# The first attention unit of an AdaLN block: another load order, maxima between projections and values, scores beside maxima

## The chip, the cores and the metric

The kernel runs on one core of a Trainium2 chip. The core has a matrix engine (TensorE, PE in the profile; its weight loads are listed apart as PEld), a vector engine (VectorE, DVE), a scalar engine (ScalarE, ACT), a general engine (GpSimd, POOL) and a queue engine that issues transfers (SyncE, SP). Each works through its own list of instructions in order and waits on semaphores of the others. The metric is device time in microseconds (us) of one execution; lower is better.

## What is computed

The reference is one transformer block with adaptive layer norm, on x of 4 batches, 1024 tokens, width 256, in float32. Cut to what matters:

```python
mod = (silu(c) @ wmod).reshape(4, 6, 1, 256)          # sa, ca, ga, sb, cb, gb
h = layernorm(x) * (1 + ca) + sa
Q, K, V = split(h @ W_qkv.T + b_qkv)                  # 16 heads of 16
attn = softmax(Q @ K.T / 4 + causal)                  # 1024 x 1024 for each head
x = x + ga * (merge(attn @ V) @ W_o.T + b_o)
h = layernorm(x) * (1 + cb) + sb
x = x + gb * moe(h)                                   # 8 experts, top 2, silu
```

The gates ga and gb are pushed away from zero to at least 0.25 in magnitude. The change lies wholly in the beginning of the attention of the first batch.

## The kernel before

**Units and steps.** The attention runs in 16 units, four per batch, each of four heads. A head has 16 channels, padded to 32 rows, so four heads fill the 128 rows of `qT` and `kT`, and four matmuls on 32 rows each can run side by side in the array. Row 16 of each group of 32 in `qT` holds the row maximum of the scores, and `kT` holds -1 there, so a score matmul already subtracts the maximum. There are three pairs of `qT`, `kT`, used in turn.

For each unit the kernel first needs maxima, then scores. Maxima come in 12 steps (`m_steps`): steps 0 to 3 are the diagonal blocks of the first half of the queries, of 512, 384, 256 and 128 keys; steps 4 to 7 take the second half against the first 512 keys; steps 8 to 11 are the diagonal of the second half. Each step is four matmuls (one per head) and four reductions on DVE. Scores also come in 12 steps (`s_steps`): four matmuls, masks on the diagonal, four exponentials on ACT, and, one step later, four products with the values (`av_step`).

In the steady loop (from L1078) a score step of unit u stands beside a maxima step of unit u+1: after each score matmul comes one maximum matmul (`m_step`, L797). There, the causal mask of a maximum is added on DVE by the fused operation of L816. `m_alone` (L835) is the form for maxima with no scores beside them: four matmuls of L848, then the mask added by PE (L854, `unit` times `qmask`), then plain reductions (L856). Nothing in it prevents the list of instructions from putting each head's mask directly behind that head's matmul, and in the first step it is laid down so.

**The start.** SP issues the two halves of x of batch 0 (L132), then wq, wk, the biases, wv, and later the other batches; ACT's queue issues the condition `sc` and the first third of the modulation's weights, `wm[0]` (L608). POOL builds constants, zeroes the three `qT`, copies wq and wk out of their padded form (L653), writes ones into both value tiles (L657), and scales the query bias (L1043). ACT fills the three `kT` (L651). DVE takes layer-norm statistics (L44, L45) tile by tile; `modulate` (L670) multiplies on PE (L676), and DVE copies the result to `modT` (L680) and adds one for the scale (L681). `ln_pieces` then gives: square root on ACT (L50), a few small DVE operations (L51 to L57), normalization of half the tokens (`xna`, L67), transposes on PE (L76), and the modulated result `hT` on ACT (L77). `xna` has one buffer.

`qk_pieces` makes projections of 256 tokens (L766) and copies them with bias on ACT (L771); column half 0 serves units 0 and 1, half 1 units 2 and 3. `spread(u)` (L779) moves projected heads into `qT` and `kT` by nine transfers on SP. `modulate_rest` (L683) computes the other two thirds of the modulation on PE (L692), copied by DVE (L693) and written to DRAM. `v_pieces` makes values of 128 tokens (L741) and adds the bias on DVE (L745). `max_rows(u, half)` (L822) transposes the finished maxima, copies them on ACT (L828) and sends them into row 16 of `qT` (L829).

**The order written out by hand** (L1039 to L1076): modulation; the layer norm of batch 0; eight projection pieces; `spread(0)`; `modulate_rest`; eight more pieces; `spread(1)`; maxima steps 0 to 3 of unit 0; a value piece; `max_rows(0, 0)`; maxima steps 4 to 7 with the other value pieces; then four times a maxima step 8 to 11 followed by a score step 0 to 3 with its own four matmuls (`four_heads`); `max_rows(0, 1)`; then maxima steps 0 to 3 of unit 1, each with a layer-norm piece of batch 1 from the list `todo`. The steady loop enters unit 0 at step 4. All PSUM tiles of this part except one come from seven banks in turn.

`in_order` (L214) pins an instruction to its place in the program's order; without it the list of an engine may be laid down otherwise.

Of the kernel before, what the change touches and what calls it, by code (L numbers as in the profile page):

```python
# [18 lines left out]
P = 128  # L19
# [42 lines left out]
def normalized(nc, pool, x_b, mv, rs, half, tag):  # L62

    xn = pool.tile([P, 4, D], F32, tag=f"xn{tag}", name=f"xn{tag}")
    for i in range(4):
        t = 4 * half + i
        nc.vector.tensor_scalar(  # L67
            xn[:, i, :], x_b[:, t, :], mv[:, t, 0:1], rs[:, t : t + 1], ALU.subtract, ALU.mult
        )
    return xn  # L70
# [10 lines left out]
def adaln_block_kernel(  # L81
# [46 lines left out]
    x_view = x.rearrange("b (t p) d -> b p t d", p=P)  # L128
    out_view = out.rearrange("b (t p) d -> b p t d", p=P)
    out_rows = out.rearrange("b t d -> (b t) d")  # L130
    for h in range(2):
        nc.sync.dma_start(out=xs[0][:, 4 * h : 4 * h + 4, :], in_=x_view[0, :, 4 * h : 4 * h + 4, :])  # L132

    ident = ctile([P, P], "ident")
    make_identity(nc, ident)
# [438 lines left out]
    with ExitStack() as actx:  # L574
# [29 lines left out]
        def load_modulation(n, eng):  # L604
            for dc in range(NDC):
                eng.dma_start(out=wm[n][dc], in_=wmod[dc * P : (dc + 1) * P, 512 * n : 512 * (n + 1)])

        load_modulation(0, nc.scalar)  # L608

        padded = []  # L610
        for name, w in (("qc", wq), ("kc", wk)):
# [35 lines left out]


        for i in range(3):
            nc.gpsimd.memset(qTs[i], 0.0)  # L650
            nc.scalar.copy(kTs[i], extra.to_broadcast([P, T]))  # L651
            if i < 2:
                nc.gpsimd.tensor_copy(  # L653
                    (wq_s, wk_s)[i].rearrange("p c (h d) -> p c h d", d=DH), padded[i][:, :, :, 0:DH]
                )
        for v in vaug:
            nc.gpsimd.memset(v[:, :, :, DH:HW], 1.0)  # L657
        zrows = dnp.tile([4, T], F32, tag="zrows", name="zrows")
# [11 lines left out]
        def modulate():  # L670

            nc.scalar.activation(sc, sc, AF.Silu)
            ps = bank("ps_m")[:, 0 : 4 * B].rearrange("p (n b) -> p n b", b=B)
            for n in range(4):
                for dc in range(NDC):
                    nc.tensor.matmul(  # L676
                        ps[:, n, :], wm[0][dc][:, n * P : (n + 1) * P], sc[:, dc, :],
                        start=(dc == 0), stop=(dc == NDC - 1),
                    )
            nc.vector.tensor_copy(modT, ps)  # L680
            nc.vector.tensor_scalar(scale1[:, 0:2, :], modT[:, 2:4, :], 1.0, None, ALU.add)  # L681

        def modulate_rest():  # L683
# [30 lines left out]
        def ln_pieces(b):  # L714
            def begin():
                st["ln", b], pieces = layer_norm_pieces(nc, small, xs[b], eps, "a")
                for f in pieces:
                    f()
                st["hT", b] = htp.tile([P, NDC, T], F32, tag="hT", name="hT")

            def piece(half, dc):
                def run():
                    if dc == 0:
                        st["xn", b] = normalized(nc, xnp, xs[b], *st["ln", b], half, "a")
                    transposed(
                        nc, misc(), st["xn", b], dc, ident,
                        st["hT", b][:, dc, half * 512 : (half + 1) * 512],
                        scale1[:, dc, b : b + 1], modT[:, dc, b : b + 1],
                    )

                return run

            out = [piece(h, dc) for h in range(NH) for dc in range(NDC)]
            return [lambda f=out[0]: (begin(), f())] + out[1:]
# [100 lines left out]
        def m_alone(u, i):  # L835

            qt, kb = m_steps[i]
            half = qt // 4
            last = kb == half
            n = (qt % 4 + 1) * P if last else 512  # L840
            kind = ("mx", u, half) if last else ("mf", u)
            if kind not in st:
                st[kind] = mxp.tile([P, 4, 4], F32, tag=kind[0], name=kind[0])
            pss = []
            for j in range(4):
                pss.append(bank("ps_max"))
                r = HW * j
                nc.tensor.matmul(  # L848
                    pss[j][:, 0:n], qTs[u % 3][r : r + HW, qt * P : (qt + 1) * P],
                    kTs[u % 3][r : r + HW, kb * 512 : kb * 512 + n], start=True, stop=not last,  # L850
                )
            if last:
                for ps in pss:
                    nc.tensor.matmul(ps[:, n - P : n], unit, qmask, start=False, stop=True)  # L854
            for j, ps in enumerate(pss):
                nc.vector.tensor_reduce(st[kind][:, j, qt % 4 : qt % 4 + 1], ps[:, 0:n], AX.X, ALU.max)  # L856

# [177 lines left out]
            for k, f in enumerate(av_step(*av)):  # L1035
                soon.append((step + 3 + 2 * k, f))


        modulate()  # L1039
        ln0, keys0 = ln_pieces(0), qk_pieces(0, 0)  # L1040
        for f in ln0:
            f()
        nc.gpsimd.tensor_scalar(bq_s, bq_s, SCALE, None, ALU.mult)  # L1043
        for f in keys0 + [spread(0), modulate_rest] + qk_pieces(0, 1) + [spread(1)]:
            f()
        values = deque(v_pieces(0))
        for i in range(4):
            m_alone(0, i)
        values.popleft()()
        max_rows(0, 0)()  # L1050
        for i in range(4, 8):
            m_alone(0, i)
            while len(values) > 7 - i:
                values.popleft()()
        blank_rows()
        st["rest"] = ln_pieces(1) + qk_pieces(1, 0), v_pieces(1) + qk_pieces(1, 1)
        todo.extend(st["rest"][0][:10])
        gates.extend(gate_pieces(0)[0])

        def four_heads(u, i):  # L1060

            pts = weigh(i, [s_step(u, i, j) for j in range(4)], True)
            if pending is not None:
                finish(pending)
            return u, i, pts

        for i in range(8, 12):
            m_alone(0, i)
            pending = four_heads(0, i - 8)
        nc.vector.tensor_tensor(st["mx", 0, 1], st["mx", 0, 1], st["mf", 0], ALU.max)  # L1070
        max_rows(0, 1)()
        for i in range(4):
            m_alone(1, i)
            todo.popleft()()
        todo.appendleft(max_rows(1, 0))
        step = 4  # L1076

        for u in range(NU):  # L1078
# [22 lines left out]
            for i in range(4 if u == 0 else 0, len(s_steps)):  # L1101
# [10 lines left out]
                    sends.extend(loads)  # L1112
                if (b, qd, i) == (B - 1, 1, 4):
                    gates.extend(weights)
                pts, scores = [], []

                if u + 1 == NU:
                    pending = four_heads(u, i)
                for j in range(4 if u + 1 < NU else 0):
                    scores.append(s_step(u, i, j))  # L1120
                    m_step(u + 1, i, (j + 2) % 4)
                    if j % 2:
                        pts.extend(weigh(i, scores[j - 1 :], j == 1))

                    if j == 1 and pending is not None:
                        finish(pending)
                if u + 1 < NU:
                    pending = u, i, pts
                    if m_steps[i] == (4, 0) and u > 0:
                        todo.appendleft(max_rows(u + 1, 0))  # L1130

                if gates:
                    gates.popleft()()
# [179 lines left out]
```

## Time and profile before

| what | us |
|---|---|
| median of 3 runs (lowest, highest) | 1100.63 (1099.53, 1101.1) |
| the profiled execution, its own time | 1096.32 |
| its span, first to last instruction | 1094.4 |
| PE busy | 1047.4 (96%) |
| DVE busy | 752.1 (69%) |
| ACT busy | 530.5 (48%) |
| POOL busy | 241.3 (22%) |

The profile is of one execution. The page gives busy time by engine, 40 slices of the span (27.4 us each) with the share of busy time in tenths, the clock that was granted to PE in tenths of full speed, the transfers, and the costliest groups of instructions by line of the code. Two readings are needed here. A busy PE is not a PE at its peak: matmuls overlap, and four matmuls on 32 rows each in one microsecond count no more than one. And the slices are too coarse for a start of some 100 us, so the order of time and the table of stretches are used: each line of the first gives start, duration, engine, line of the code, operation, output and input, count, and in brackets how long the engine had stood idle and for whom.

Where the start stands in that order:

| us | event |
|---|---|
| 4.95 | first layer-norm statistics |
| 7.37 | first modulation matmul |
| 20.51 | first transposes of normalized tokens |
| 58.80 | the run of value projections begins |
| 71.95 | first score matmul |
| 83.67 | transposes of the second half's maxima |

The mean granted clock over the execution is 0.979 of full speed.

### The profile page before, as it was taken

What the parts mean: (1) busy time and instruction counts of PE and PEld (TensorE: products, weight loads), DVE (VectorE), ACT (ScalarE), POOL (GpSimd) and SP (SyncE); (2) the same over time, 40 slices, a digit from 0 to 9 for tenths busy, and PEclk for the clock granted to TensorE, in tenths of its full rate; (3) what the DMA queues carried; (4) which work ended last, traced back from release to release, by engine and by line L of the source; (5) the groups of instructions that cost most, each with busy time, mean ns of one, the idle gap of its engine ahead of it and who ended that gap; (6) DMA issues with size and microseconds to landing.
All of it is one profiled execution on the core that took longest, in us unless ns stands there. A gap on an engine that the chain in (4) does not pass through costs nothing. (4 is left out here: it accounts for less than half of the span.)

```text
span 1094.4 us, 23062 instructions
## 1 busy us (share of the span) xinstructions
PE 1047.4 (96%) x8202; PEld 589.2 (54%) x8202; DVE 752.1 (69%) x2326; ACT 530.5 (48%) x1153; POOL 241.3 (22%) x233
## 2 busy tenths in 40 slices
PE   3999999999999999999999999999799999999994
PEld 3554434444444353444445444443277888889884
DVE  5766767667777868767786778786246777666662
ACT  3224655566655455665545555444632254445540
POOL 4000010000000001330000133113213574454444
PEclk9898999999999999999999999989999999999997
DMA  8220111101102110231202113001458966443432
GB/s 274 46 55 7 31 27 37 30 17 38 30 21 75 37 40 15 74 72 40 59 15 42 45 52 100 26 22 50 142 180 265 352 154 146 78 65 64 74 63 24
DMA packets 68690, 81.61 MB, mean 75 GB/s; under 512 B 19480, under 2 KB 50072, under 8 KB 68448
## 3 DMA queue, kind: packets, MB, share of 16 engines
q1 hardware_dynamic: 54720, 62.73, 21.0%
q0 software_dynamic: 13296, 16.89, 8.7%
q8 instruction: 64, 1.05, 0.4%
q10 hardware_dynamic: 560, 0.53, 0.1%
q14 instruction: 50, 0.41, 0.1%
HBM read 45.11 MB, written 24.93 MB: 64 GB/s over the span
## 5 line engine op out<-in xcount | busy, mean ns | idle before, releaser
L888 ACT ACTIVATE pt<-ps_s 128x512 f32<-128x512 f32 (+3 forms) x768 | 334.3, 489 | 321.3 <-PE ps_s L883 206.7
L805 PE MATMUL ps_max<-kT,qT 32*128 32x512 f32 (+3 forms) x1408 | 387.9, 540 | 1.3 <-DVE mx L816 0.7
L867 PE MATMUL ps_s<-qT,kT 32*128 32x512 f32 (+3 forms) x1536 | 365.2, 539 | 2.7 <-DVE qc L535 2.1
L867 PEld LDWEIGHTS ps_s<-qT,kT 32*128 32x128 f32 x1536 | 127.9, 185 | 164.7 <-issue 70.3
L812 DVE TENSOR_REDUCE mf<-ps_max 128x1 f32<-128x512 f32 x240 | 154.2, 685 | 54.6 <-PE ps_max L805 51.2
L900 PE MATMUL av<-pt,vaug 128*32 128x512 f32 (+3 forms) x1536 | 164.6, 497 | 2.1 <-ACT ot L908 1.0
L816 DVE CUSTOM_DVE_ANT_0 unused<-ps_max,cmask,mf 128x512 f32<-128x512 f32 (+3 forms) x240 | 131.6, 548 | 46.7 <-PE ps_max L805 23.2
L932 POOL TENSOR_TENSOR oc<-oc,rec 64x512 f32<-64x512 f32 x32 | 40.8, 1274 | 540.7 <-DMA rec<-inv 423.8
L805 PEld LDWEIGHTS ps_max<-kT,qT 32*128 32x128 f32 x1408 | 142.0, 184 | 24.6 <-DVE mx L816 10.2
L816 DVE CUSTOM_DVE_ANT_0 unused<-ps_max,cmask 128x512 f32<-128x512 f32 (+3 forms) x224 | 109.9, 491 | 59.4 <-PE ps_max L805 34.0
L564 POOL DMA_INDIRECT out_dram<-y,xb x67 | 106.5, 1590 | 124.4 <-DVE gs L526 39.9
L547 PE MATMUL ps_h<-xt,wa 128*128 128x256 f32 (+1 forms) x608 | 123.6, 355 | 1.1 <-DVE xt L535 1.1
L558 PE MATMUL ps_y<-wb,hs 128*128 128x256 f32 x536 | 122.8, 379 | 1.0 <-ACT hs L551 1.0
L547 PEld LDWEIGHTS ps_h<-xt,wa 128*128 128x128 f32 x608 | 102.5, 191 | 11.6 <-DVE xt L535 1.3
L558 PEld LDWEIGHTS ps_y<-wb,hs 128*128 128x128 f32 x536 | 100.6, 190 | 14.4 <-ACT hs L551 1.4
L883 PEld LDWEIGHTS <-qmask 128*32 128x32 bf16 (+1 forms) x1352 | 30.1, 95 | 109.4 <-issue 102.0
L526 DVE SCALAR_TENSOR_TENSOR gs<-x,share,gs 128x256 f32<-128x256 f32 x201 | 85.2, 479 | 1.0
L340 POOL DMA_INDIRECT slots<-hr,sloti x64 | 64.0, 1000 | 89.5 <-ACT sloti L339 52.2
L551 ACT ACTIVATE hs<-ps_h 128x512 f32<-128x512 f32 x67 | 39.8, 597 | 87.3 <-PE ps_h L547 85.8
L563 DVE TENSOR_TENSOR y<-ps_y,gs 128x256 f32<-128x256 f32 x67 | 26.0, 420 | 73.2 <-PE ps_y L558 66.8
L883 PE MATMUL ps_s<-unit,qmask 128*32 128x128 bf16 (+1 forms) x1352 | 72.9, 226 | 0.0
L900 PEld LDWEIGHTS av<-pt,vaug 128*32 128x32 f32 x1536 | 34.1, 110 | 53.6 <-issue 39.4
(223 smaller groups left out, 988.1 us busy)
## 6 DMA issues: line engine op xcount, KB each, us to landing
w_s<-in_w_dram SPq DMA_DIRECT2D x16, 512.0 KB
xb<-slots SPq DMA_DIRECT2D x29, 259.0 KB
qT<-qc SPq DMA_DIRECT2D x64, 64.0 KB
kT<-kc SPq DMA_DIRECT2D x64, 64.0 KB
oc<-ot SPq DMA_DIRECT2D x128, 32.0 KB
rec<-inv SPq DMA_DIRECT2D x32, 128.0 KB
out_dram<-x SPq DMA_DIRECT2D x8, 512.0 KB
wa<-in_w_dram SPq DMA_DIRECT2D x8, 512.0 KB
```

The costliest lines, as they stand in the source:

```text
L340: sent = nc.gpsimd.indirect_dma_start(out=slots, out_offset=bass.IndirectOffsetOnAxis(ap=at, axis=0), in_=hr[:, t, :], in_offset=None,).ins
L526: nc.vector.scalar_tensor_tensor(gs[:, j, :], gb[:, b, :], share[:, j, b : b + 1], gs[:, j, :], ALU.mult, ALU.add)
L547: nc.tensor.matmul(ps[:, k, :], w[:, dc, fc * P : (fc + 1) * P], xt[:, dc, :], start=(dc == 0), stop=(dc == NDC - 1),)
L558: nc.tensor.matmul(ps[:, j, :], hs[:, fc, j * P : (j + 1) * P], w[:, fc, :], start=(fc == 0), stop=(fc == NFC - 1),)
L564: added = nc.gpsimd.indirect_dma_start(out=out_rows, out_offset=bass.IndirectOffsetOnAxis(ap=xb[:, j, D : D + 1].bitcast(I32), axis=0), in ...
L805: nc.tensor.matmul(ps[:, 0:n], qTs[u % 3][r : r + HW, qt * P : (qt + 1) * P], kTs[u % 3][r : r + HW, kb * 512 : kb * 512 + n], start=True, ...
L812: nc.vector.tensor_reduce(st["mf", u][:, j, qt - 4 : qt - 3], ps, AX.X, ALU.max)
L816: nc.vector.tensor_tensor_reduce(out=unused[:, 0:n], in0=ps[:, 0:n], in1=cmask[:, 512 - n : 512], scale=1.0, scalar=st["mf", u][:, j, qt - ...
L867: nc.tensor.matmul(ps[:, 0:n], kTs[u % 3][r : r + HW, kt * P : (kt + 1) * P], qTs[u % 3][r : r + HW, qb * 512 + r0 : (qb + 1) * 512], star ...
L883: nc.tensor.matmul(ps[k : k + w, 0:P], qmask[:, k : k + w], unit, start=False, stop=True)
L888: nc.scalar.activation(pt[:, 0:n], ps[:, 0:n], AF.Exp)
L900: nc.tensor.matmul(av[HW * j : HW * (j + 1), r0:512], vaug[b % 2][:, kt, 4 * qd + j, :], pts[j][:, 0 : 512 - r0], start=(kt == 0), stop=(k ...
```

## The change

Loads: x's first half goes first; `wm[0]` moves from ACT's queue to SP, between the halves of x.

Engines: the copies of wq and wk move from POOL to ACT, the first between the modulation's silu and the square root; of the `kT` fills one stays ahead of the projections' copies and two are written after twelve projection pieces; the bias scaling on POOL moves forward and is pinned behind the first zeroing of `qT`. The copy of the modulation to `modT` and its scale move behind the normalization of the first half.

Order: after eight projection pieces and `spread(0)` come four more pieces, then `modulate_rest`; the last four pieces, `spread(1)` and the eight value pieces are placed between maxima steps 0 to 7 of unit 0. In `m_alone` the first mask is pinned, so that the four matmuls stand together ahead of the masks. Maxima steps 8 to 11 of unit 0 now run beside score steps 0 to 3 by a new function `both`, the body of the steady loop; they therefore use `m_step` and DVE's mask. Layer-norm pieces of batch 1 stand there too. Of unit 1's maxima, step 0 follows `max_rows(0, 1)` and steps 1 to 3 move into steps 4 to 6 of unit 0; `max_rows(1, 0)` goes to step 7.

```diff
-    for h in range(2):
+    def load_first(h):
         nc.sync.dma_start(out=xs[0][:, 4 * h : 4 * h + 4, :], in_=x_view[0, :, 4 * h : 4 * h + 4, :])
+    load_first(0)
...
-        load_modulation(0, nc.scalar)
+        load_modulation(0, nc.sync)
+        load_first(1)
...
         for i in range(3):
-            nc.gpsimd.memset(qTs[i], 0.0)
-            nc.scalar.copy(kTs[i], extra.to_broadcast([P, T]))
-            if i < 2:
-                nc.gpsimd.tensor_copy(
-                    (wq_s, wk_s)[i].rearrange("p c (h d) -> p c h d", d=DH), padded[i][:, :, :, 0:DH]
-                )
+            in_order(nc.gpsimd.memset(qTs[i], 0.0))
+            if i == 0:
+                in_order(nc.gpsimd.tensor_scalar(bq_s, bq_s, SCALE, None, ALU.mult))
...
-            nc.vector.tensor_copy(modT, ps)
+            return ps
+        def modulated(ps):
+            in_order(nc.vector.tensor_copy(modT, ps))
             nc.vector.tensor_scalar(scale1[:, 0:2, :], modT[:, 2:4, :], 1.0, None, ALU.add)
...
                         st["xn", b] = normalized(nc, xnp, xs[b], *st["ln", b], half, "a")
+                        if b == 0 and half == 0:
+                            modulated(st.pop("ps_m"))
...
-                for ps in pss:
-                    nc.tensor.matmul(ps[:, n - P : n], unit, qmask, start=False, stop=True)
+                for k, ps in enumerate(pss):
+                    mask = nc.tensor.matmul(ps[:, n - P : n], unit, qmask, start=False, stop=True)
+                    if k == 0:
+                        in_order(mask)
...
+        def both(u, i, u_max, i_max):
+            pts, scores = [], []
+            for j in range(4):
+                scores.append(s_step(u, i, j))
+                m_step(u_max, i_max, (j + 2) % 4)
+                if j % 2:
+                    pts.extend(weigh(i, scores[j - 1 :], j == 1))
+                if j == 1 and pending is not None:
+                    finish(pending)
+            return u, i, pts
+        st["ps_m"] = modulate()
+        ln0 = ln_pieces(0)
+        ln0[0]()
+        for w, w_s in zip(padded, (wq_s, wk_s)):
+            nc.scalar.copy(w_s.rearrange("p c (h d) -> p c h d", d=DH), w[:, :, :, 0:DH])
+        nc.scalar.copy(kTs[0], extra.to_broadcast([P, T]))
+        keys1 = qk_pieces(0, 1)
+        for f in ln0[1:] + qk_pieces(0, 0) + [spread(0)] + keys1[:4]:
+            f()
+        for i in (1, 2):
+            nc.scalar.copy(kTs[i], extra.to_broadcast([P, T]))
+        modulate_rest()
+        fill = deque(keys1[4:] + [spread(1)] + v_pieces(0))
+        for i in range(8):
+            m_alone(0, i)
+            for _ in range((2, 2, 2, 1, 2, 2, 1, 1)[i]):
+                fill.popleft()()
+            if i == 3:
+                max_rows(0, 0)()
...
-        for i in range(8, 12):
-            m_alone(0, i)
-            pending = four_heads(0, i - 8)
-        nc.vector.tensor_tensor(st["mx", 0, 1], st["mx", 0, 1], st["mf", 0], ALU.max)
+        for i in range(4):
+            pending = both(0, i, 0, 8 + i)
+            todo.popleft()()
         max_rows(0, 1)()
-        for i in range(4):
-            m_alone(1, i)
-            todo.popleft()()
-        todo.appendleft(max_rows(1, 0))
+        m_alone(1, 0)
...
+                pending = both(u, i, u + 1, i) if u + 1 < NU else four_heads(u, i)
+                if u == 0 and 4 <= i < 7:
+                    m_alone(1, i - 3)
+                if u + 1 < NU and i == (4 if u > 0 else 7):
+                    todo.appendleft(max_rows(u + 1, 0))
```

As the lists are laid down, ACT's is: silu, wq copy, first `kT` fill, square root, wk copy, the other two fills, `hT`; POOL's is: zeroing of the first `qT`, ones of one value tile, bias scaling, zeroing of the other two `qT`, ones of the other value tile.

## The prediction

> **What bounds the kernel now.** I read the page first, then the first 150 us in stretches of 5 us, then the order of time for 0 to 140 us, then the waits of that stretch.
>
> The page's slices show TensorE (PE) at nine tenths nearly everywhere after the first slice:
>
> ```profile
> PE   3999999999999999999999999999799999999994
> PEclk9898999999999999999999999989999999999997
> ...
> L805 PE MATMUL ps_max<-kT,qT 32*128 32x512 f32 (+3 forms) x1408 | 387.9, 540 | 1.3 <-DVE mx L816 0.7
> L867 PE MATMUL ps_s<-qT,kT 32*128 32x512 f32 (+3 forms) x1536 | 365.2, 539 | 2.7 <-DVE qc L535 2.1
> ```
>
> The two large matmul groups wait under 3 us in all, so from the steady loop on PE's queue sets the time and whatever the first unit gains or loses should arrive at the end undiminished. In the built order of the changed kernel every engine but SP is identical to before from step 8 of unit 0 on, and SP differs only in its opening loads. So I forecast one date: when PE reaches step 8 of unit 0, **113.9 us before** (a step in the order of time that begins at 113.88 with L867 and L805).
>
> How that date comes about is in the order of time (start, duration, engine, instruction):
>
> ```profile
> 11.90 0.17 DVE L680 COPY modT<-ps_m 128x16 f32<-128x16 f32 x1 [5.80 <-PE ps_m L676]
> 12.08 3.55 POOL L657 MEMSET vaug<- 128x2048 f32 x2
> 12.15 3.50 DVE L681 TENSOR_SCALAR scale<-modT 128x8 f32<-128x8 f32 x1
> 17.27 1.28 ACT L50 ACT_TABLE_LOAD   x1 [9.56 <-DVE mva L45]
> 19.95 1.38 DVE L67 TENSOR_SCALAR xna<-x,mva,rsa 128x256 f32<-128x256 f32 x4
> 24.88 1.12 PE L766 MATMUL ps_mi<-hT,wq_s 128*128 128x256 f32 x4
> 31.97 3.60 PE L692 MATMUL ps_g<-wm,sc 128*4 128x512 f32 x8
> 35.63 0.65 DVE L693 COPY mod<-ps_g 4x512 f32<-4x512 f32 x1
> 42.60 1.12 PE L848 MATMUL ps_max<-kT,qT 32*128 32x512 f32 x2
> 46.89 0.69 DVE L856 TENSOR_REDUCE mx<-ps_max 128x1 f32<-128x512 f32 x1 [1.06 <-PE ps_max L854]
> 71.96 2.48 DVE L856 TENSOR_REDUCE mx<-ps_max 128x1 f32<-128x512 f32 x4
> 93.13 1.06 PE L867 MATMUL ps_s<-qT,kT 32*128 32x512 f32 x1
> ```
>
> DVE stands for 5.80 us in front of the modulation copy while layer-norm statistics queue behind it; its next instruction, 8 elements wide, takes 3.50 us because POOL's memsets are running. Projections start at 24.88. The first maxima (42.60) go one head at a time, and then PE runs at half clock:
>
> ```profile
> 45.00:50.00 5.00, 5.00 (x15) 1.51 (x14) 2.08 (x3) 0.00 (x0) 0.00 (x0) 0.55 0.15 26
> 50.00:55.00 5.00, 5.00 (x37) 3.14 (x30) 3.83 (x11) 0.00 (x0) 0.00 (x0) 0.50 0.00 0
> 55.00:60.00 5.00, 5.00 (x18) 2.49 (x18) 1.96 (x6) 1.54 (x2) 0.00 (x0) 0.58 0.26 99
> 95.00:100.00 5.00, 5.00 (x25) 1.91 (x24) 2.67 (x6) 3.10 (x5) 0.00 (x0) 0.50 0.00 0
> ```
>
> Columns: stretch, then busy of PE, PE loads, DVE, ACT, POOL; the granted clock stands third from the end. By single microseconds the low clock lasts from 45.3 to 59.1 and from 93.3 to 100.1.
>
> **1. Loads and first layer norm: projections start at 20.2 instead of 24.9, gain 4.7.** The ring now carries x's first half, the two wm tiles, x's second half, wq, wk, 524 kB each. The DMA view of the first 62 us (1.55 us a slice) moved 178, 687, 1288, 1872, 2472 kB by 3.1, 4.65, 6.2, 7.75, 9.3 us. Before, wq ended the first 2.1 MB, 8.35 us on this curve, and its copy began at 9.19: 0.85 from byte to use. On the same curve: first half 5.0, wm 6.4, second half 7.8, wq 9.2, wk 10.5. Moving wm from ACT's queue to SP costs two issues of 0.52 there; SP's later loads wait for bytes, not issues, so nothing more. L676's 16 matmuls (7.37 to 11.87 before) end near 10, and their copy and scale (0.17 each) now lie between the two halves of `xna`, where DVE idled 1.31 for PE: hidden. The statistics run without a break: four tiles of 0.39 after 7.8, done by 9.5. ACT is later: it now holds the wq copy (POOL's row: 0.61) and one kT fill (1.03), from 9.2 to 10.8; then table load 1.28 and square root 0.30, 12.4. The wk copy and two kT fills (0.61+2×1.03) follow to 15.1, before the first `hT` falls due near 17 (`xna` to `hT` took 2.05): hidden, up to 2.7 if the normalization came earlier. Five small DVE instructions (18.90 to 19.95 before, 1.05) make it 13.5.
>
> Here a rule is weighed. POOL now waits for bq behind wk (the DMA rate dips from 9.3 to 10.85, the small pieces; about 11), then runs three memsets, 0.95+0.95+1.81, to about 15.0. The Trainium skill, "SBUF — State Buffer", on the shared port pair, says that a two-port VectorE instruction and a GpSimd one exclude each other for the whole instruction. By that, the small tensor_scalar L56 (due 12.9) waits for the memset in progress, under 1 us. The row above says more: 3.50 us spans **both** back-to-back memsets, 1.81 each. By the row it waits to 15.0 and `xna` starts at 15.3. I take the row. From `xna` to the first projection took 24.88−19.95=4.93: **S = 20.2** (18.4 with no collision).
>
> **2. From S to the first reduction.** PE: eight projection pieces (31.83−24.88=6.95), four of the next pair (3.5), L692 (3.6): S+14.05. The q/k copies into qT, kT (SP issues 31.71 to 37.90, plus some 2 to land) come at S+15, so PE can begin maxima then. DVE cannot: after the second L693 copy it needs 8.05 (35.63 to 43.69), now less two of eight statistics, 7.3. **First reduction at S+21.3.** PE idles some 3 us there, a wait the change creates; the ACT projections behind the last square root wait as well.
>
> **3. Maxima with projections and values.** Eight maxima steps and eight values: with the masks after four concurrent matmuls, a 512 step is 1.07+0.33 instead of 6.4 (42.60 to 49.00). DVE: reductions 2.48, 1.95, 1.42, 0.88, then 4×2.48, and eight value adds of 0.41. Before, at full clock, one step and one value took 2.73 (63.78 to 66.51), DVE without a gap. Sum 19.5; PE's share (four projections 3.5, values 8.5, steps 8.4, less 3.1 done early) is 17.3, beside it. DVE ends at S+40.8=61.0; before, 71.96. From S: 40.8 against 47.1, **gain 6.3**.
>
> **4. First scores beside maxima.** Before: 71.96 to 93.13, 21.2. After: four double steps. The same steps in a later unit took 12.8 (156.2 to 169.0) at PE's limit; one value product less (−1.05), four layer-norm pieces of 0.61 more (+2.4), PE starting 1.6 ahead of DVE: 12.9, and DVE's own sum is 10.6 of custom maxima and 2.9 of `xna`, equal (the mask matmuls of the maxima go, being DVE's cmask in these steps). A **new wait** follows: `max_rows(0,1)` needs DVE's last maximum, a transpose (0.28), a copy (0.24), an 8 kB DMA (issue 0.59; a similar one, inv at 114.76, released its successor at 116.2), before step 4's scores; only one maxima step (1.4) lies between. I take 3.4. Total 16.3, **gain 4.9**.
>
> **5. Steps 4 to 7.** Before 93.13 to 113.88, 20.75, of which half clock costs 3.4. After: four steps of 4.2 (105.48 to 109.68) plus three maxima steps moved in here (1.2+0.9+0.65, with waits 3.5): 20.4, **gain 0.3**.
>
> Sum 4.7+6.3+4.9+0.3 = 16.2. The rule on idle gaps speaks against this: "TensorE: Matmul & The Clock Gate" (why this matters for your kernels) says that no gap above some 3 us may stand between bursts, else half clock. The trace's granted clock shows no drop for the 8.6 us idle before 20.5, but both drops follow thin work (single-head maxima; small maxima waiting on DVE). By the rule the waits in 2 and 4 each cost a period of 6.8 us at half clock, 3.4 each; by the rows nothing. Part 3 is DVE's, so a drop there costs 17.3+3.4−19.5=1.2. I take that one, nothing in 4: **gain 15**.
>
> Against its own time of 1096.3 (span 1094.4 and 1.9 around it) the profile would show about 1081; the median of the runs shown lies 4.3 above it: **1085.5**.
>
> **Rivals.** (a) Half the gain: both new waits cost a full low-clock period, the row DMA lands a microsecond later, DVE's custom maxima fall behind by 2: 15−3.4−1−2=8.6, **1092**. For it: the waits are real; against: the steady loop, equally built, never drops.
> (b) Slower: the low clock holds through parts 3 and 4, since interleaving leaves PE waiting on DVE all along. 17.3 and 14 us of PE work double; 17.3+17.3−19.5=15.1 plus 14 is 29 lost, **1115**. It decides once more than about 32 us beyond part 3's slack run at half clock. Against: 63 to 86 us held full clock in just such DVE-paced work.
> (c) No POOL collision, clock whole: +1.8+1.2, **1082.5**.
> (d) The start is hidden anyway: batch loads (DMA busy to 27.9) hold DVE's other statistics, so only parts 3 to 5 count: 10.3, **1090**.
>
> Chances: forecast 0.50, (a) 0.15, (b) 0.09, (c) 0.14, (d) 0.09, 0.03 for no difference. Range 1080 to 1094; outside it are (b) and little else. Under 0.2% (2.2 us) a measurement cannot tell from none: faster 0.88, same 0.03, slower 0.09.
>
> **What would show it.** Right: first L766 near 20, first L856 near 41.5 and bunched in fours, step 8 near 98.5. Wrong in 1: no DVE instruction stretched beside memsets, or one longer. Wrong in 3 or 4: granted clock 0.5 between 62 and 80, or PE waiting for rows over 3 us before the first unmasked scores. The whole is wrong if step 8's gain does not reach the end.

## The result and the profile after

The changed kernel takes 1088.42 us (median of 4 runs, 1087.28 to 1089.52) against 1100.16 in the same runs for before: ratio **0.9892**, interval 0.9875 to 0.9910. It is 11.7 us faster, where the forecast was 15 and 1085.5. The profiled execution was one of the slower ones: 1089.52 us, span 1087.8.

The lines of the page that answer to those of before (the first two are 40 slices of the span; the others give count, busy time and mean, then the idle time and its releaser):

```profile
PE   5999999999999999999999999999799999999994
PEclk9899999999999999999999999899999999999998
...
L812 PE MATMUL ps_max<-kT,qT 32*128 32x512 f32 (+3 forms) x1440 | 396.5, 537 | 1.3 <-DVE mx L823 1.1
L876 PE MATMUL ps_s<-qT,kT 32*128 32x512 f32 (+3 forms) x1536 | 364.9, 538 | 3.5 <-DVE qc L538 2.1
```

The steady loop is as before; the first slice went from 3 to 5 tenths. The start in the order of time (start, duration, engine, instruction, idle time before it), first DVE's list:

```profile
14.02 1.77 DVE L56 TENSOR_SCALAR nwa<-nwa 128x8 f32<-128x8 f32 x1
...
16.02 1.38 DVE L67 TENSOR_SCALAR xna<-x,mva,rsa 128x256 f32<-128x256 f32 x4
...
24.68 0.75 DVE L44 BATCH_NORM_STATS2 sta<-x 128x6 f32<-128x256 f32 x2 [4.59 <-DMA x<-in_x_dram]
...
30.42 0.20 DVE L51 RECIPROCAL rsa<-rsa 128x8 f32<-128x8 f32 x1 [1.70 <-ACT rsa L50]
...
43.13 2.48 DVE L865 TENSOR_REDUCE mx<-ps_max 128x1 f32<-128x512 f32 x4
46.38 1.95 DVE L865 TENSOR_REDUCE mx<-ps_max 128x1 f32<-128x384 f32 x4 [0.77 <-PE ps_max L861]
50.87 1.42 DVE L865 TENSOR_REDUCE mx<-ps_max 128x1 f32<-128x256 f32 x4 [2.54 <-PE ps_max L861]
...
66.09 0.41 DVE L752 TENSOR_TENSOR vaug<-ps_mi,bv_s 128x256 f32<-128x256 f32 x1
```

then PE's:

```profile
20.95 1.77 PE L773 MATMUL ps_mi<-hT,wq_s 128*128 128x256 f32 x4
22.55 1.03 PE L773 MATMUL ps_mi<-hT,wk_s 128*128 128x256 f32 x4
...
35.67 2.65 PE L855 MATMUL ps_max<-kT,qT 32*128 32x512 f32 x8
...
43.87 2.25 PE L855 MATMUL ps_max<-kT,qT 32*128 32x384 f32 x6 [2.60 <-DVE mx L865]
...
46.45 2.02 PE L773 MATMUL ps_mi<-hT,wq_s 128*128 128x256 f32 x4
48.26 1.76 PE L773 MATMUL ps_mi<-hT,wk_s 128*128 128x256 f32 x4
...
81.71 0.66 PE L876 MATMUL ps_s<-qT,kT 32*128 32x512 f32 x1 [0.52 <-DMA qT<-rows]
...
101.94 0.69 PE L876 MATMUL ps_s<-qT,kT 32*128 32x512 f32 x1
```

and the stretches of 5 us around the low clock (the granted clock is third from the end):

```profile
40.00:45.00 5.00, 2.40 (x9) 1.32 (x9) 4.67 (x21) 1.03 (x3) 0.00 (x0) 0.79 0.49 84
45.00:50.00 5.00, 5.00 (x21) 2.91 (x16) 2.56 (x6) 0.47 (x1) 0.00 (x0) 0.53 0.15 26
```

At the very start this column can't be used. It reads 1.00 up to 22.5 us, but the four projection matmuls at 20.95 took 0.60 us each, as long as those from 46.45 on, where the column shows half clock, and the next ones 0.38. So PE ran at half speed there although the column does not show it. "Low clock" below means what the column shows.

The dates of before in the next table that are not shown yet are these:

```profile
43.92 0.69 DVE L856 TENSOR_REDUCE mx<-ps_max 128x1 f32<-128x512 f32 x1 [0.24 <-PE ps_max L854]
...
71.63 0.41 DVE L745 TENSOR_TENSOR vaug<-ps_mi,bv_s 128x256 f32<-128x256 f32 x1
...
113.88 0.69 PE L867 MATMUL ps_s<-qT,kT 32*128 32x512 f32 x1
```

PE projects 3.93 us earlier and brings its first maximum 6.93 us earlier (42.60 to 35.67). But DVE stands from 20.1 to 24.68 for batch 1's x, and its first reduction comes only 0.79 earlier (43.92 to 43.13). PE then stands for DVE, 2.60 us. The low clock, 20.5 us long in all before 110 us in the kernel before, is 6.8 us here (43 to 50). Four stages make up the gain at step 8 of unit 0, where PE begins at 101.94 instead of 113.88:

| stage | before | after | gain |
|---|---|---|---|
| to DVE's first reduction | 43.92 | 43.13 | 0.79 |
| from there to the end of DVE's last value add (72.04; 66.50) | 28.12 | 23.37 | 4.75 |
| from there to step 4's first score (93.13; 81.71) | 21.09 | 15.21 | 5.88 |
| steps 4 to 7 | 20.75 | 20.23 | 0.52 |
| sum | 113.88 | 101.94 | 11.94 |

Of the 11.94, 11.30 are still there when unit 1's second maxima are transposed (130.35 and 119.05), and some 10.7 at 675 us. In this execution low clock periods late in the span (around 678 and 787 us) then lose more than before's did; only 6.6 are left between the two spans, but the medians differ by 11.7.

### The profile page after: what moved, and what is told of

It is laid out like the page before. It is cut to its first block, busy times and chain, and to the rows that moved or that the text cites. A ratio compares the mean times of both kernels' runs of the same rounds, so it can differ in the third digit from the quotient of the medians.

```text
span 1087.8 us, 23015 instructions
## 1 busy us (share of the span) xinstructions
PE 1038.7 (95%) x8162; PEld 586.9 (54%) x8162; DVE 752.9 (69%) x2341; ACT 531.9 (49%) x1155; POOL 240.8 (22%) x231
## 5 line engine op out<-in xcount | busy, mean ns | idle before, releaser
L812 PE MATMUL ps_max<-kT,qT 32*128 32x512 f32 (+3 forms) x1440 | 396.5, 537 | 1.3 <-DVE mx L823 1.1
L823 DVE CUSTOM_DVE_ANT_0 unused<-ps_max,cmask,mf 128x512 f32<-128x512 f32 (+3 forms) x256 | 140.3, 548 | 49.2 <-PE ps_max L812 24.4
L812 PEld LDWEIGHTS ps_max<-kT,qT 32*128 32x128 f32 x1440 | 145.7, 184 | 25.6 <-DVE mx L823 10.9
L561 PEld LDWEIGHTS ps_y<-wb,hs 128*128 128x128 f32 x536 | 100.6, 190 | 13.7 <-ACT hs L554 0.7
L554 ACT ACTIVATE hs<-ps_h 128x512 f32<-128x512 f32 x67 | 39.8, 597 | 87.5 <-PE ps_h L550 76.5
```

The source lines that it names most:

```text
L561: nc.tensor.matmul(ps[:, j, :], hs[:, fc, j * P : (j + 1) * P], w[:, fc, :], start=(fc == 0), stop=(fc == NFC - 1),)
L812: nc.tensor.matmul(ps[:, 0:n], qTs[u % 3][r : r + HW, qt * P : (qt + 1) * P], kTs[u % 3][r : r + HW, kb * 512 : kb * 512 + n], start=True, ...
L823: nc.vector.tensor_tensor_reduce(out=unused[:, 0:n], in0=ps[:, 0:n], in1=cmask[:, 512 - n : 512], scale=1.0, scalar=st["mf", u][:, j, qt - ...
```

## The experiments

Eleven kernels, each timed beside the kernel before. The theory at the outset: DVE's statistics of the other batches, which wait for their loads, hide the start; the interleaving and the scores beside maxima earn the time. Ratios are to before; "step 8" is PE's date in the profiled execution.

| run | projections | batch 1's statistics | first reduction | last value add ends | step 8 | ratio (interval) |
|---|---|---|---|---|---|---|
| before | 24.88 | 23.94 | 43.92 | 72.04 | 113.88 | 1 |
| changed | 20.95 | 24.68 | 43.13 | 66.50 | 101.94 | 0.9892 (0.9875 to 0.9910) |
| loads_back | 21.70 | 23.31 | 41.83 | 65.53 | 100.61 | 0.9885 (0.9865 to 0.9906) |
| maxima_back | 20.18 | 24.18 | 43.09 | 66.05 | 101.52 | 0.9913 (0.9891 to 0.9934) |
| scores_back | 20.17 | 23.29 | 42.82 | 66.37 | 108.03 | 0.9943 (0.9923 to 0.9962) |
| start_alone | 20.50 | 24.66 | 43.90 | 67.36 | 110.20 | 0.9956 (0.9938 to 0.9974) |
| interleave_alone | 24.83 | 23.89 | 44.14 | 64.98 | 109.50 | 0.9951 (0.9929 to 0.9973) |
| before_x_early | 25.31 | 19.66 | 45.06 | 71.62 | 116.12 | 1.0006 (0.9987 to 1.0026) |
| x_early | 19.86 | 18.92 | 38.41 | 59.23 | 94.64 | 0.9834 (0.9814 to 0.9854) |
| x_early_pool_first | 19.21 | 18.26 | 36.95 | 57.78 | 93.14 | 0.9826 (0.9795 to 0.9857) |
| x_early_serial | 20.07 | 19.14 | 40.20 | 61.07 | 96.54 | 0.9849 (0.9815 to 0.9883) |
| pool_first | 18.26 | 23.12 | 40.10 | 62.20 | 97.55 | 0.9869 (0.9829 to 0.9910) |
| keep_busy | 20.10 | 23.98 | 41.76 | 63.90 | 99.24 | 0.9888 (0.9854 to 0.9922) |

**Taking parts away from the changed kernel.** loads_back undoes the opening loads:

```diff
-        load_modulation(0, nc.sync)
-        load_first(1)
+        load_modulation(0, nc.scalar)
...
     load_first(0)
+    load_first(1)
```

> The changed kernel with only the opening loads undone: both halves of x first, wm on ACT's queue. Theory (the start's gain does not come from the loads and is mostly covered): the square root stays behind the wq copy on ACT, so the first projection stays within 1 us of 20.95; DVE still waits for the x of batch 1 near 24.7, so the first reduction stays at 43.1 plus or minus 0.6 and step 8 at 101.9 plus or minus 1.5; time within 2 us of the changed kernel's 1088.4. Rival (step 1 of the prediction: the order of the loads gives the start its gain, and the gain reaches the end): first projection at 23 or later, step 8 at 104 to 106, time 1091 to 1093.

1086.63 us. The rival falls: the order of the loads earns nothing that can be seen (ratios 0.9885 and 0.9892). The first projection is 0.75 later, yet the first reduction is 1.30 *earlier*, outside what was expected, because batch 1's x is used 1.37 earlier. One execution each cannot say how much of that is the 512 kB that left SP's ring.

maxima_back puts the first maxima and values back:

```diff
-        for f in ln0[1:] + qk_pieces(0, 0) + [spread(0)] + keys1[:4]:
+        for f in ln0[1:] + qk_pieces(0, 0) + [spread(0)]:
...
-        fill = deque(keys1[4:] + [spread(1)] + v_pieces(0))
...
+        for f in keys1 + [spread(1)]:
+            f()
+        values = deque(v_pieces(0))
```

> The changed kernel with the first eight maxima steps and the values in the old order (all projections first, mask behind each head, values in the second half). Theory (the interleaving itself gives the gain): from first reduction to DVE's last value add 28 us instead of 23.4, step 8 at 106 to 107, time 1092 to 1094. Rival (the gain is the granted clock): the low clock between 40 and 65 us lasts 13 us or more instead of 6.8, and without its 3.4 us the stage would be as short as in the changed kernel.

Both fall. 1088.41 us, step 8 at 101.52: taking the interleaving away cost nothing that can be seen there (the ratio is 0.0021 higher, with overlapping intervals). The low clock was 6.8 us long again, and from first reduction to last value add took 22.96. DVE's list says why:

```profile
43.09 6.88 DVE L863 TENSOR_REDUCE mx<-ps_max 128x1 f32<-128x512 f32 x16
```

All sixteen reductions run without a gap. In the kernel before the same sixteen took from 43.92 to 55.4, with waits of 0.52, 1.06, 1.53 and 1.12 for PE between them. Here PE had begun its first maximum at 38.65, four microseconds before DVE was free. One reservation: without the pin the list of PE happened to put four matmuls ahead of the masks, so this run did not test the form of one head at a time; start_alone does.

scores_back restores the old scores part:

```diff
-        for i in range(4):
-            pending = both(0, i, 0, 8 + i)
-            todo.popleft()()
-        max_rows(0, 1)()
-        m_alone(1, 0)
+        for i in range(8, 12):
+            m_alone(0, i)
+            pending = four_heads(0, i - 8)
+        nc.vector.tensor_tensor(st["mx", 0, 1], st["mx", 0, 1], st["mf", 0], ALU.max)
+        max_rows(0, 1)()
+        for i in range(4):
+            m_alone(1, i)
+            todo.popleft()()
```

> The changed kernel with the first scores part in the old form (maxima steps 8 to 11 with PE's mask, then four scores with their own matmuls, unit 1's maxima in a block ahead of step 4). Theory (scores beside maxima give the gain by themselves): from DVE's last value add (66.5) to step 4 21 us instead of 15.2, step 8 at 107 to 109, time 1094 to 1095, with or without a low clock period. Rival (the gain of this part is the low clock period that went): without a low clock period between 70 and 110 us step 8 is at 104 to 105 and the time 1091; with one it is 3.4 later.

1093.43 us. The last value add ends at 66.37 and step 4 begins at 87.28: 20.9 us, before's 21.1 again. The low clock came back too:

```profile
85.00:90.00 5.00, 5.00 (x23) 2.35 (x21) 2.43 (x9) 0.71 (x2) 0.00 (x0) 0.75 0.01 3
90.00:95.00 5.00, 5.00 (x25) 1.53 (x25) 2.95 (x7) 2.73 (x5) 0.00 (x0) 0.57 0.01 1
```

but it begins near 87.5, after step 4 has started, so the 5.7 us by which the stage up to step 4 is longer are not the clock's. They are this:

```profile
70.12 1.95 DVE L865 TENSOR_REDUCE mx<-ps_max 128x1 f32<-128x384 f32 x4 [1.36 <-PE ps_max L861]
73.67 1.42 DVE L865 TENSOR_REDUCE mx<-ps_max 128x1 f32<-128x256 f32 x4 [1.61 <-PE ps_max L861]
76.46 0.88 DVE L865 TENSOR_REDUCE mx<-ps_max 128x1 f32<-128x128 f32 x4 [1.37 <-PE ps_max L861]
79.54 4.40 DVE L865 TENSOR_REDUCE mx<-ps_max 128x1 f32<-128x512 f32 x8 [1.98 <-PE ps_max L861]
```

Columns as above. PE and DVE take turns, 6.3 us of waits, and then a block of unit 1's maxima stands ahead of step 4. With this part undone the kernel is 5 to 6 us slower (1093.43 less 1088.42, or 0.0051 in the ratios; 6.09 at step 8). Theory and rival are not parted by it. In steps 4 to 7 scores_back has a low period of 6.8 us, worth up to 3.4, and the changed kernel has unit 1's maxima there instead. Without that period step 8 would stand near 104.6, which leaves some 2.7 of the 6.09 to the order of work, and the rival had said 104 to 105 and 3.4 more with such a period. All five kernels with the old scores part show a low period between 85 and 106 us and none of the eight with the new one does. How much of the gain is the clock's is open.

**One part alone, on the kernel before.** start_alone is the new start with the old order after it, its first step's masks pinned behind each head:

```diff
+                if last and (u, i) == (0, 0):
+                    in_order(nc.tensor.matmul(pss[j][:, n - P : n], unit, qmask, start=False, stop=True))
```

> The start of the changed kernel (loads, ACT's copies, modulation between the halves) with everything after it in the order of before: all projections first, the first step's masks one head at a time and pinned so, values in the second half, the old scores part. Theory (start and interleaving replace each other: with the start about 4 us earlier PE does the first maxima while DVE is still at the statistics, so their form no longer matters): first reduction at 42.8 to 43.5, DVE's last value add at 65.5 to 67.5 instead of 71.96, step 8 within 1.5 us of the run with only the scores undone (108.0), time 1092.5 to 1095. Rival (the prediction's sum, where the interleaving has a gain of its own of 6): DVE's last value add at 70 or later, step 8 at 111 or later, time 1097 or more.

interleave_alone is the kernel before with the new order of the first maxima and the pinned mask:

```diff
-        for f in keys0 + [spread(0), modulate_rest] + qk_pieces(0, 1) + [spread(1)]:
+        keys1 = qk_pieces(0, 1)
+        for f in keys0 + [spread(0)] + keys1[:4] + [modulate_rest]:
             f()
+        fill = deque(keys1[4:] + [spread(1)] + v_pieces(0))
```

> The kernel before with only the first maxima interleaved and their first mask pinned; its start and its scores part stay. Theory (start and interleaving replace each other): first reduction at 43.5 to 44.5 as before, DVE's last value add at 66 to 68.5 instead of 71.96, step 8 at 108 to 110.5 instead of 113.9, so alone it is worth 4 to 6 us although its removal from the changed kernel cost nothing; time 1093 to 1096 against before's 1098.5. Rival (the interleaving is worth nothing at all): DVE's last value add at 71 or later, time within 1.5 us of before.

1096.17 and 1095.70 us, before 1099.93 beside them. Alone the start brings the last value add from 72.04 to 67.36, the interleaving to 64.98 (1.0 earlier than expected; the only one of the three without a low period in that stage); both together (scores_back) to 66.37, no further than one alone. They replace each other, as expected: either brings PE's maxima ahead of DVE's first reduction, by an earlier start or by putting projections off, and what is behind DVE is hidden. start_alone came 2.2 later at step 8 than scores_back, 0.7 over its range, and its time is 1.2 over; its low clock lasted 20.5 us in the first 110, scores_back's 13.7, and half of the 6.8 between them is 3.4. The rival, a gain of its own of 6, falls.

**Feeding DVE earlier.** x_early moves loads only, those of batches 1 to 3 and of the rest of the modulation's weights, ahead of wv and wo:

```diff
+        nc.sync.dma_start(out=xs[1], in_=x_view[1])
+        for n in (1, 2):
+            load_modulation(n, nc.sync)
+        for b in range(2, B):
+            nc.sync.dma_start(out=xs[b], in_=x_view[b])
         wv_s = load(wv.rearrange("(c p) n -> p c n", p=P), [P, NDC, D], "wv_s")
...
-        for n in (1, 2):
-            load_modulation(n, nc.sync)
...
-        for b in range(1, B):
-            nc.sync.dma_start(out=xs[b], in_=x_view[b])
```

> The changed kernel with one thing more: the x of batch 1 is loaded right behind the biases, then the rest of wm, then the x of batches 2 and 3, and only then wv and wo. Theory (the first reduction hangs on the statistics of the other batches, which wait for their loads, 24.68 us in the changed kernel): batch 1's x lands near 15, DVE's statistics run without that 4.6 us wait, the first reduction comes at 38.5 to 39.5 instead of 43.1, PE no longer stands there, and step 8 comes at 97 to 99; time 1083.5 to 1086. Rival (PE's own work or the low clock sets that stage): first reduction earlier, but DVE's last value add stays at 66.5 plus or minus 1 and the time within 1.5 us of 1088.4.

1079.71 us, better than expected: **6 to 9 us faster than the changed kernel** (0.9892 less 0.9834, of 1098.5, is 6.4; the two medians, from different sets of runs, lie 8.7 apart). DVE's list:

```profile
17.62 1.38 DVE L67 TENSOR_SCALAR xna<-x,mva,rsa 128x256 f32<-128x256 f32 x4 [1.02 <-PE ps_mi L76]
18.92 0.74 DVE L44 BATCH_NORM_STATS2 sta<-x 128x6 f32<-128x256 f32 x2
...
38.41 4.39 DVE L865 TENSOR_REDUCE mx<-ps_max 128x1 f32<-128x512 f32 x8
```

The statistics follow the normalization without the wait of 4.59, the first reduction comes 4.7 earlier, and the stage behind it is 2.55 shorter (20.82 for 23.37). The clock stays whole over the stretch where it had been halved:

```profile
40.00:45.00 5.00, 5.00 (x41) 3.15 (x38) 4.19 (x11) 0.95 (x2) 0.00 (x0) 1.00 0.56 95
45.00:50.00 5.00, 5.00 (x36) 3.10 (x33) 4.00 (x12) 1.54 (x2) 0.00 (x0) 1.00 0.37 121
```

before_x_early does the same to the kernel before.

> The kernel before with only the batches' x loaded early. Theory (there PE arrives at its maxima at 42.6 and takes them one head at a time, so DVE's loads did not bind): first reduction at 43 to 44, step 8 within 1.5 us of 113.9, time within 2 us of before. Rival (the batch loads bind in both kernels): first reduction at 40 or earlier, step 8 at 110 or earlier, time 1095 or less.

1100.24 us against 1099.93: nothing, as expected. Two dates of its trace lie outside what was expected: the first reduction at 45.06 and step 8 at 116.12, 2.2 later than in before. Batch 1's statistics begin at 19.66 there, ahead of the normalization, the first projection comes 0.4 later and PE's first maximum 1.1 later (43.74), and the low clock lasted 23.9 us instead of 20.5. DVE is ready earlier and stands for PE:

```profile
45.06 0.69 DVE L856 TENSOR_REDUCE mx<-ps_max 128x1 f32<-128x512 f32 x1 [4.29 <-PE ps_max L854]
```

The loads bind only once PE has been made early. x_early_serial joins x_early and maxima_back.

> The run with the batches' x loaded early, with the first eight maxima and the values in the old order. Theory (once DVE is no longer late, PE's order decides again): PE reaches its first maximum near 37.5 behind four more projections, DVE's last value add comes at 61 to 65 instead of 59.15, step 8 2 to 6 us later than 94.6, time 1081.5 to 1086 against 1079.7. Rival (the order never matters behind the new start): DVE's last value add at 58.5 to 60, step 8 within 1 us of 94.6.

1080.35 us, ratio 0.9849; x_early's interval covers it. In the trace the order costs 1.84 at the last value add and 1.90 at step 8, just under the 2 to 6 that the theory gave there; the time, below the expected range, is not told apart from x_early's.

**The start after all?** POOL's memsets ahead of the bias scaling, so that none stands beside DVE's L56:

```diff
             in_order(nc.gpsimd.memset(qTs[i], 0.0))
-            if i == 0:
-                in_order(nc.gpsimd.tensor_scalar(bq_s, bq_s, SCALE, None, ALU.mult))
         for v in vaug:
-            nc.gpsimd.memset(v[:, :, :, DH:HW], 1.0)
+            in_order(nc.gpsimd.memset(v[:, :, :, DH:HW], 1.0))
+        in_order(nc.gpsimd.tensor_scalar(bq_s, bq_s, SCALE, None, ALU.mult))
```

> The changed kernel with POOL's five memsets ahead of the bias scaling, and the loads as they are. Theory (behind the start DVE waits for the x of batch 1, so an earlier start alone gains nothing): L56 at 0.2 us, first projection at 19 to 19.7 instead of 20.95, but the first reduction stays at 43.1 plus or minus 0.6 and step 8 at 101.9 plus or minus 1.2, time within 1.5 us of the changed kernel. Rival (the start counts in full): first reduction and step 8 1.3 to 1.8 us earlier, time 1086 to 1087.

> The run with the batches' x loaded early, and POOL's five memsets now ahead of the bias scaling, so that none of them waits for the bias's load. Theory (the 1.7 us that the small DVE operation L56 takes beside a memset delays everything behind it, now that no load does): L56 takes 0.17 to 0.2, the first projection comes at 18 to 18.5 instead of 19.9, the first reduction and step 8 1.2 to 1.8 earlier than 38.41 and 94.6, time 1 to 3 us under that run's 1079.7. Rival (memsets that run earlier slow down the statistics or the DVE work between 7 and 12 us instead, or the load of batch 1 holds again): L56 short but the first projection within 0.6 of 19.9, or the first reduction within 0.5 of 38.41; time unchanged within 1.

Here the theory fell in part. On the changed kernel the first reduction came at 40.10, 3 us earlier, and step 8 at 97.55; the theory had said unchanged, the rival 1.3 to 1.8. Batch 1's statistics began 1.56 earlier, and DVE's waits between there and the first reduction shrank from 1.86 to 0.40, nearly all of it the wait for the square root on ACT. So the start does reach DVE by a second way: ACT is through with its projections earlier. The load's own date is the other part: over the six profiled executions with the changed kernel's loads it ranged from 23.12 to 24.68, and why is open. On x_early it was 1.46 at the first reduction and 1.50 at step 8, as expected (the first projection, at 19.21, came 0.7 later than expected), but not in the time: 1081.24 against 1079.71, ratios 0.0008 apart. pool_first's ratio, 0.9869, also overlaps the changed kernel's.

**The clock.** keep_busy adds three matmuls where PE stands for DVE (2.60 us, from 41.27 to 43.87):

```diff
+            if i == 0:
+                warm = ps_av.tile([P, 512], F32, tag="av", name="av")
+                for k in range(3):
+                    in_order(nc.tensor.matmul(
+                        warm.rearrange("p (t d) -> p t d", d=D), ident, xs[0][:, 0:2, :],
+                        start=k == 0, stop=k == 2,
+                    ))
```

> The changed kernel with three extra matmuls of 128 by 512 (some 2.7 us at full clock; their result is never used) placed in PE's queue where it stands idle from about 41 to 43.9 us for DVE's first reduction; nothing else is changed. Theory (the low clock period from 43 to 50 us is the answer to that idle PE): no low clock between 40 and 60 us, DVE's waits of 0.77 and 2.54 us in the maxima shrink by 2 to 3 us in all, step 8 at 98.5 to 100.5 instead of 101.9, time 1 to 3 us under the changed kernel's. Rival (the periods come whatever PE does there): a low clock period of 6.8 us between 40 and 60 us again, step 8 at 101.5 to 103, time unchanged or up to 1 us longer.

Inconclusive: the ratio is 0.9888, as without. The low clock came from 37.6 to 41, *ahead* of the added work (41.71 to 44.38), and 3.4 long instead of 6.8:

```profile
37.00:38.00 1.00, 1.00 (x4) 0.29 (x2) 1.00 (x6) 0.00 (x0) 0.22 (x1) 0.81 0.06 16
38.00:39.00 1.00, 1.00 (x6) 0.57 (x6) 1.00 (x7) 0.00 (x0) 0.44 (x2) 0.50 0.09 16
...
41.71 2.74 PE L1088 MATMUL av<-x,ident 128*128 128x512 f32 x6
```

Neither view had that. Step 8 at 99.24 is in the theory's range, but 1.37 of the 2.70 had been gained before the first reduction. What sets off a period is not shown.

## Why the prediction was right

The time, 1088.4, lies in the range of 1080 to 1094, 2.9 above the forecast, and the sign and the place were right: everything is won before step 8, and 11.3 of the 11.9 there outlast the first unit. The range alone proves little. It also holds rivals (a), (c) and (d), and 11.9 at step 8 is nearer to (d)'s 10.3 than to 15. By steps:

1. **Start.** 20.95 against 20.2 said; 20.1 to 20.95 over the five profiled executions that share the start and the loads. Loads came about 1 us later than the curve gave (wq's copy at 10.17, said 9.2; the bias scaling at 11.98, said 11), so the memsets ended at 15.76, said 15.0. L56 waited for that end, 1.77 us. Here the row chosen and the page's rule give the same, for only one memset was left when L56 came; the last section shows what parts them. The load order, to which the sum gave its first lines, earns nothing (loads_back).
2. **Another step that failed: "First reduction at S+21.3".** It came at S+22.2 (43.13, not 41.5). The size was nearly right, and by luck. The second L693 copy (L698 now) came at 35.88, S+14.9 for S+14.05 said, mostly because the first four projections still ran at half speed (1.60 to the next four, in before 0.95). From the copy to the reduction took 7.25, said 7.3. But the copy is not what DVE hung on. DVE had first to take batch 1's x, whose load had not moved earlier, and from 30.42 on it worked almost without a gap. In loads_back the copy came at 35.91 and the reduction 5.92 behind it, in x_early at 35.31 and 3.10 behind it. The prediction's rival (d), the start hidden by batch loads, names this; x_early against before_x_early shows it. Here 3.1 of the start's 3.9 us were lost, where the forecast had 2.3 of 4.7.
3. **The step that failed most: maxima and values, "Sum 19.5", taken without a gap on DVE.** 19.5 and 1.2 for the clock were said, 23.37 came. DVE's own work was right: 19.07. Its waits for PE, set at nothing but those 1.2, were 4.30. In the four runs without a low clock period here (interleave_alone, x_early, x_early_pool_first, x_early_serial) they were 1.8 and the stage took 20.82 to 20.87; in the seven with one of 3.4 to 10.2 us in it or just ahead, 22.10 to 23.70. The largest wait, 2.54, stands behind two projections that took 2.02 and 1.76 at half clock; in x_early the same two took 1.08 and 1.03. Before itself and before_x_early, where single heads are exposed as well, took 28.12 and 26.56. But before's low clock covers 13.7 us of its stage; half of that taken off leaves 21.3, so most of this stage's gain may be the clock's. The prediction also missed that start and interleaving replace each other.
4. **Scores.** 16.3 was said, 15.21 came. The new wait was over-priced: rows were written at 79.58 and used at 81.71, with PE idle 0.52 for them and busy with unit 1's first maxima until then. 3.4 had been set aside.
5. **Steps 4 to 7.** 20.4 said, 20.23 came.

In sum: the forecast, with its 1.2 for the clock, had the last value add at 62.2, and it ended at 66.50, 4.3 late: 0.7 from the start, 0.9 up to the first reduction, 2.7 in the maxima. 1.1 came back in the scores and 0.2 in steps 4 to 7. That is the 3 us between the 15 said and the 11.94 measured at step 8.

Smaller slips of the working do not carry it: the two matmul groups of the page stand idle 4.0 us in all, not under 3; part 3's terms as listed add up to 19.9, not 19.5; part 4's give 12.6, not 12.9. One reading does matter for the clock: "no drop for the 8.6 us idle before 20.5" was taken from the column that cannot be used there. Behind that gap a transpose of L76 took 0.43 us on average in before, and 0.28 in the changed kernel between 67 and 79 us at full clock.

**The clock's share.** The prediction counted before's low clock inside its stage times and took it out only in part 5 (3.4). Each run lists its mean granted clock; from 1 minus that mean, times twice the span, comes the time at half clock. Over 51 runs of the kernel before, each set about its own mean, this goes with most of the spread of 1093 to 1106 (correlation 0.90, 0.35 us of time for each us at half clock). The mean is 51 us in those runs and 35 in the four of the changed kernel; at 0.35 that goes with 5.6 of the 11.7. In x_early it is 23, which goes with 4.3 more. Both are estimates from that slope. How much of it the changes cause is open, though x_early, x_early_pool_first and x_early_serial show no low clock in the first 110 us at all, and the other ten kernels each show some. The Trainium skill, "TensorE: Matmul & The Clock Gate" (What's actually happening), describes a free-running window of 3.41 us by which the clock is judged: every period in these traces but the last of each, which runs to the end of the span, is 3.4, 6.8, 10.2 or 13.7 long, which agrees. Its rule that an idle gap above some 3 us brings half clock (Why this matters for your kernels), which the forecast set aside, does not account for the periods around 40 us: in the changed kernel PE stood 2.60 us and the low clock began at 43.0, 1.7 us into that gap, and in keep_busy it began with PE busy, and no gap over 0.8 us had come since the projections began. The slow transposes behind the gap of 8.6 us in before agree with it, but no run shows that the gap caused them.

## What to carry to other kernels

When an engine's work is moved earlier, look up what the *other* engine stands for in the same stretch before counting the gain: here 3.9 us of start were worth 0.8 at the first reduction until loads were moved as well, and those loads, moved alone, were worth nothing. Two edits that both hide the same engine behind another replace each other; test each with the other taken away before keeping both. Price a stretch by its own clock, and check the clock's column against the durations of equal instructions: one kernel's executions spread over 13 us, most of it along with the granted clock, more than a small edit moves.

## What the runs showed of the hardware

Not every DVE instruction waits for a POOL memset. With the memsets early (pool_first), statistics and their aggregates ran beside them at 0.39 to 0.40 and 0.17 as elsewhere, and only an 8-element TENSOR_SCALAR was held (with L382 behind it in DVE's queue), through the rest of one memset and the whole of the next (POOL's row, then DVE's):

```profile
8.54 3.54 POOL L658 MEMSET vaug<- 128x2048 f32 x2
```

```profile
8.94 0.40 DVE L44 BATCH_NORM_STATS2 sta<-x 128x6 f32<-128x256 f32 x1
...
9.59 2.52 DVE L49 TENSOR_SCALAR vea<-mva 128x8 f32<-128x8 f32 x1
```

It ended at 12.11, the memsets at 12.08. So the wait is not for the memset in progress alone, which is the reading that the prediction took from before's row (3.50 us over two memsets). Ahead of the square root that wait is covered: the next DVE instruction still stood 0.24 for ACT.
